# Turning layer-norm rows by VectorE blocks and SBUF copies instead of TensorE transposes, and two heads' probabilities by one VectorE instruction, in a cross-attention block

## The chip, the cores and the metric

One core of one Trainium2 chip runs the whole kernel. The metric is the device time of one execution in microseconds (us). TensorE multiplies, VectorE and ScalarE work on tiles in SBUF and PSUM, GpSimd does a few additions, and SyncE issues nearly all DMA transfers. In the profile these are PE (PEld for its weight loads), DVE, ACT, POOL and SP (SPq for what SP's own queue does).

## The reference

Four sequences, each with 512 query rows x and 512 context rows, width 512, 16 heads of 32, all in fp32. The mask is all true in these inputs, but it is applied.

```python
x = layer_norm(hidden_states, ln1_w, ln1_b)
q = (x @ q_w + q_b)...; k = (enc @ k_w + k_b)...; v = (enc @ v_w + v_b)...
scores = where(mask, q @ k.T * scale, mask_value)
out = softmax(scores) @ v
hidden = out @ cproj_w + cproj_b + hidden_states
y = layer_norm(hidden, ln2_w, ln2_b)
y = gelu(y @ fc_w + fc_b) @ proj_w + proj_b          # inner width 2048
return hidden + y
```

layer_norm is the usual one: mean and variance over the 512 columns, then a weight and a bias per column.

## The kernel before

**Units.** The attention part has 16 groups w = 4b + g: sequence b, four heads g. Each group has four query tiles qt of 128 rows; unit u = 4w + qt. For each unit, TensorE computes the scores of four heads into one PSUM tile (`scores`, line 279); VectorE adds the mask and takes the minimum of the negated scores by row (284); ScalarE takes the exponential and the row sum (288); and VectorE turns the probabilities in 32x32 blocks into a tile tb (`turn`, lines 302 and 310). Two units make a pair, p = 2w + half. After a pair's second unit, 16 copies, 32 partitions each, carry its blocks from tb to the transposed tile pT (`copies`, line 345); `attend` (362) multiplies pT by v, and VectorE scales the result (367).

**One pT.** Pairs 1, 3, 5, 7 and 25 to 31 have buffers of their own (in gt and xe). All others share one tile pT: the copies of the next such pair are emitted just after the attend that frees it. Pairs 8 to 23 attend at the start of unit 2p + 4, so pair 9 at unit 22, pair 16 at 36, pair 23 at 50.

**Other work in between.** After scores and turn, each unit runs some chains of about 3.4 us of TensorE: projections of k, q and v for later groups (kN, qN, vN for group N; lines 235, 245, 257), the output projection cproj of the previous sequence (403), and parts of its MLP (fc at 469, proj at 479). What runs where is written out by hand in the lists `first` and `later`: a tuple gives each unit its own list, while a plain list is spread over the four units by cost in the loop at the end (`run` takes work while what is spent plus half the next cost fits the budget). Transposes are counted at 0.5 each.

**Order.** The schedule is manual: each engine executes what the program emits, in order, and waits in order. SyncE's queue too: a DMA that waits for a tile holds all DMAs emitted after it, weights, rows of x and the copies of pairs among them.

**Layer norms.** There are eight: the first norm of each sequence (giving xT, the input of q), and the second (giving yT, the input of fc). For each: statistics and normalisation by rows in four tiles (`ln_stat`, `ln_rs`, `ln_norm`; lines 145 to 167), then `ln_turn`: 16 TensorE transposes (176) into four PSUM tiles, and weight and bias on the way out, by VectorE (179) or ScalarE (181). The normalised tiles come from a pool of four, which also holds the loaded rows of x (`load_x`, line 194), of h for the next residual (`load_h`, 391) and of the second norm's input (`load_xn`, 412). In the attention part the norms are turned in unit 20 (first norm of sequence 2), 21 to 23 (second norm of 0), 32 to 34 (first of 3) and 46, 47 (second of 1); the second norms of 2 and 3 are turned in the last part (`last_mlps`), each between the second and the third product of a projection, after which the sums over yT (line 501, ys) follow.

Of the kernel before, what the change touches and what calls it, by code (L numbers as in the profile page):

```python
# [1 line left out]

# [9 lines left out]
F32 = mybir.dt.float32  # L38
U8 = mybir.dt.uint8
AF = mybir.ActivationFunctionType  # L40
# [5 lines left out]
P = 128  # L46
B, L, D, H = 4, 512, 512, 16
HD = D // H
INNER = 4 * D
NT = L // P  # L50
ND = D // P
NG = ND
HG = H // NG
# [3 lines left out]
NI = P // HD  # L57
# [15 lines left out]
LN1W, LN1B, QB, KB, LN2W, LN2B, FCB = 0, 4, 8, 12, 16, 20, 24  # L73
# [4 lines left out]
def xattn_block(ctx: ExitStack, tc: tile.TileContext, x, encT, mask, q_w, k_w, v_w, c_w, fc_w, p_w, vecs, rows, out):  # L78
    nc = tc.nc
    scale = float(np.float32(1.0) / np.sqrt(HD).astype(np.float32))  # L80

    def pools(stack, **bufs):
        return [stack.enter_context(tc.tile_pool(name=n, bufs=k)) for n, k in bufs.items()]

    const, keep, hids, tiles, small = pools(ctx, const=1, keep=1, hids=6, tiles=4, small=4)
    dram = ctx.enter_context(tc.tile_pool(name="dram", bufs=1, space=bass.MemoryType.DRAM))
    ps_acc = ctx.enter_context(tc.tile_pool(name="ps_acc", bufs=4, space=PSUM))

# [34 lines left out]
    def score_tile():  # L123
# [2 lines left out]
        n = n // 2 * 4 + n % 2  # L126
        return ptt[:, n * D : (n + 1) * D]

    def kqv_w(w, i):
        n = 4 * i + 2 + w % 2  # L130
        return ptt[:, n * D : (n + 1) * D].rearrange("p (d f) -> p d f", d=ND)

    S = {}
    count = [0, 0, 0]
    Q = [nc.sync]

    def acc_tile(name):
# [33 lines left out]
    def ln_turn(key, d, xn, dst):  # L171

        w, bi = (LN1W, LN1B) if key[0] == 1 else (LN2W, LN2B)
        tp = acc_tile(f"tp{key[0]}_{key[1]}_{d}")
        for t in range(NT):
            nc.tensor.transpose(tp[:, ts(t, P)], xn[t][:, ts(d, P)], ident)
        wd, bd = vec[:, w + d : w + d + 1], vec[:, bi + d : bi + d + 1]
        if d in (1, 2) and key not in BY_ACT:
            nc.vector.tensor_scalar(dst[:, d, :], tp, wd, bd, ALU.mult, ALU.add)
        else:  # L180
            nc.scalar.activation(dst[:, d, :], tp, AF.Identity, bias=bd, scale=wd)


    def queue(b):
        return Q[0] if b else nc.sync

    def load_enc(b):
        for d in range(ND):
            queue(b).dma_start(out=eT[:, d, :], in_=encT[b, ts(d, P), :])

    def load_x(b):
        S["xn", b] = [tiles.tile([P, D], F32, tag="xn", name=f"xn1_{b}_{t}") for t in range(NT)]
        for t in range(NT):
            queue(b).dma_start(out=S["xn", b][t], in_=x[b, ts(t, P), :])

# [76 lines left out]
    def scores(w, qt):  # L272
        if qt == 0:
            S["sums", w] = small.tile([P, NT, HG], F32, tag="sums", name=f"sums_{w}")
        qT, kT, sums = S["qT", w], S["kT", w], S["sums", w]
        sc = ps_sc.tile([P, HG, L], F32, tag="sc", name=f"sc_{w}_{qt}")
        for h in range(HG):
            r = slice(h * HD, (h + 1) * HD)
            nc.tensor.matmul(sc[:, h, :], qT[r, ts(qt, P)], kT[r, :], start=True, stop=True)  # L279
        ps = []  # L280
        for h in range(HG):
            s = score_tile()
            mn = small.tile([P, 1], F32, tag="mn", name=f"mn_{w}_{qt}_{h}")
            nc.vector.tensor_tensor_reduce(  # L284
                out=s, in0=sc[:, h, :], in1=S["mb", w // NG], scale=1.0, scalar=FMAX,
                op0=ALU.add, op1=ALU.min, accum_out=mn,
            )
            nc.scalar.activation(s, s, AF.Exp, bias=mn, scale=-1.0, accum_out=sums[:, qt, h : h + 1])  # L288
            ps.append(s)
        S["ps", w, qt] = ps  # L290

    def turn(w, qt):

        half, q = divmod(qt, 2)
        if q == 0:


            S["tb", w, half] = two.tile([P, NI, PW + 2 * HD], F32, tag="tb", name=f"tb_{w}_{half}")
        tb = S["tb", w, half]
        tv = tb[:, :, :PW].rearrange("p j (a t h q) -> p a h t j q", a=2, t=NT, h=HG)  # L300
        for h in range(HG - q):
            nc.vector.transpose(tv[:, q, h], S["ps", w, qt][h])  # L302
        if q == 0:
            return

        rs = small.tile([P, 2, HG], F32, tag="rsum", name=f"rsum_{w}_{half}")
        nc.vector.reciprocal(rs, S["sums", w][:, 2 * half : 2 * half + 2, :])
        rr = one.tile([P, 2, HG, HD], F32, tag="rr", name=f"rr_{w}_{half}")
        nc.scalar.copy(rr, rs[:, :, :, None].broadcast_to([P, 2, HG, HD]))
        nc.vector.transpose(tv[:, q, HG - 1], S["ps", w, qt][HG - 1])  # L310
        nc.vector.transpose(
            tb[:, :, PW:].rearrange("p j (a q) -> p a j q", a=2), rr.rearrange("p a h d -> p (a h d)")
        )
        waiting.append((w, half))
        if w < NW - 1 or half == 0:
            exchange()
# [59 lines left out]
    def stays(b, t):  # L376

        return b == 0 or b == SPLIT and t < 2

    def load_h(b, *ts_):  # L380

        if ("xa", b) not in S:
            S["xa", b] = dram.tile([L, D], F32, tag=f"xa{b}", name=f"xa{b}")
        for t in ts_:
            if b == B - 1:

                S["h", b, t] = k_q(t // 2, t % 2)
            else:
                pool, tag = (hids, "hid") if stays(b, t) else (tiles, "xn")
                S["h", b, t] = pool.tile([P, D], F32, tag=tag, name=f"h_{b}_{t}")  # L390
            Q[0].dma_start(out=S["h", b, t], in_=x[b, ts(t, P), :])
            if stays(b, t):
                S["hid", b, t] = S["h", b, t]
# [14 lines left out]
    def load_xn(b):  # L408

        for t in range(NT):  # L410
            S["h", b, t] = tiles.tile([P, D], F32, tag="xn", name=f"hn_{b}_{t}")
            Q[0].dma_start(out=S["h", b, t], in_=S["xa", b][ts(t, P), :])

    def load_hid(b, ts_):
# [10 lines left out]

    def norm2(b, t):
        h = S["h", b, t]
        y = tiles.tile([P, D], F32, tag="xn", name=f"xn2_{b}_{t}") if stays(b, t) else h
        S.setdefault(("yn", b), {})[t] = y
        ln_norm((2, b), t, y, h)  # L430

# [2 lines left out]
            if stays(b, t):  # L434
                add_row(S["hid", b, t], 1)

    def ln2_turn(b, d):
        if d == 0:
            S["yT", b] = keep.tile([P, ND, L], F32, tag="yT", name=f"yT_{b}")
        ln_turn((2, b), d, S["yn", b], S["yT", b])  # L440


    weights, products = [], []
# [268 lines left out]
    CHAIN, TURN = 3.4, 0.5  # L712

    def do(fn):
        return [(0.0, fn)]

    def A(w):
        if w >= NW:
            return []
        return [  # L720
            (CHAIN, lambda: prep_k(w)),
            (CHAIN, lambda: prep_q(w)),
            (CHAIN, lambda: prep_v(w)),
        ]

    def C(b):
        return [(CHAIN, lambda t=t: cproj(b, t)) for t in range(NT)]

    def turns1(b):
        return [(TURN, lambda d=d: ln1_turn(b, d)) for d in range(ND)]  # L730

    def turns2(b):
        return [(TURN, lambda d=d: ln2_turn(b, d)) for d in range(ND)]

    def FC(b, q):
        return [(CHAIN, lambda f=f: fc(b, f)) for f in range(q * FQ, (q + 1) * FQ)]
# [3 lines left out]

    def inputs(b):
        ln = [(0.0, lambda part=part: ln1(b, part)) for part in range(3)]
        return do(lambda: load_x(b)), ln, turns1(b), do(lambda: load_enc(b))

    def run(work, budget=None):

# [62 lines left out]
    def some(n):  # L809
        taken, mlp[:n] = mlp[:n], []  # L810
        return taken
# [4 lines left out]
    def h_(b, *ts_):  # L816
        return do(lambda: load_h(b, *ts_))
# [4 lines left out]
    def pb_(b):  # L822
        return do(lambda: proj_bias(b))

    def rs(b):
        return do(lambda: ln_rs((2, b)))

    def stat(b, *ts_):
        return do(lambda: [stat2(b, t) for t in ts_])

    def norm(b, *ts_):
        return do(lambda: [norm2(b, t) for t in ts_])


    x1, x2, x3, x4 = inputs(2)
    k, q, v = A(7)
    c, t2 = C(0), turns2(0)
    first[4] = x1 + [k, q, v] + x4
    later[4] = c[:1] + x2[:1] + c[1:2] + x2[1:2] + c[2:3] + x2[2:] + c[3:]
    k, q, v = A(8)  # L840
    first[5] = (
        [k] + stat(0, 0, 1, 2, 3) + rs(0) + x3 + norm(0, 0, 1, 2, 3) + [v], [q] + t2, some(2) + pb_(0), some(2)
    )
    k, q, v = A(9)
    x1, x2, x3, x4 = inputs(3)
    first[6] = [k, q] + some(4) + [v] + x1
    k, q, v = A(10)
    first[7] = [k, q] + x2[:1] + some(2) + x2[1:2] + some(3) + [v]

    k, q, v = A(11)  # L850
    first[8] = h_(1, 0, 1) + x2[2:] + [k, q] + x3[:2] + some(1) + x3[2:3] + [v] + x3[3:] + h_(1, 2, 3) + x4
    later[8] = cb(1) + C(1)
    k, q, v = A(12)
    first[9] = [q] + some(2) + [k] + some(2) + [v]
    k, q, v = A(13)
    first[10] = [k, q] + some(4) + [v]
    k, q, v = A(14)
    t2 = turns2(1)
    first[11] = (
        [k, q] + stat(1, 0, 1, 2, 3) + rs(1), some(2) + norm(1, 0, 1, 2, 3), some(1) + t2[:2] + [v],  # L860
        t2[2:] + pb_(1) + some(1) + h_(2, 2, 3, 0, 1)
    )

# [101 lines left out]
```

## Time and profile before

| | |
|---|---|
| time, three runs | 809.81, 810.5, 810.87 us; median 810.5 |
| the profiled execution | span 810.8 us from its first to its last instruction; the page gives no other time of it |
| TensorE | 794.0 us busy (98%) |
| VectorE, ScalarE, GpSimd | 556.1 (69%), 359.8 (44%), 98.5 us (12%) |
| SyncE's DMA queue (q1) | 132.43 MB, 61.3% of 16 DMA engines' time |
| layer-norm transposes (line 176) | 128 |
| turns of probabilities (lines 302, 310) | 224 of mean 683 ns, 32 of 656 ns, each 128 x 512 |
| pair copies (line 345) | 504 from SyncE, 8 from ScalarE, 136 KB each |

Lines of the timeline read: start, duration, engine, line, operation, out<-in, count, and in brackets the idle time before with what ended it; the chain of waits has start, duration, what. A line of the windows holds a stretch and its length, busy time (and instructions) of PE, PEld, DVE, ACT and POOL, the granted TensorE clock, the DMA engines' busy share and GB/s. A line for one source line has the shortest, median and longest duration in ns, and the first and last start.

### The profile page before, as it was taken

Reading aid. Unit: us, or ns where it says so; the run is one execution under the profiler, and the core shown is the slowest. Engines: PE = TensorE matmul, PEld = TensorE weight load, DVE = VectorE, ACT = ScalarE, POOL = GpSimd, SP = SyncE. Lnnn points to the kernel's source line nnn. Section 1 sums busy time; section 2 is a strip of 40 time slices with the busy share of each in tenths; the row PEclk is TensorE's granted clock in tenths of the full one; section 3 lists DMA queues with packets and bytes.
Section 4 is the critical chain, followed back from the end, with each engine's and each line's share of the span. In section 5 each row is a group of like instructions: output and inputs, shape, how many; then the busy total and the mean of one; then the engine's idle time right before and its main releaser. Section 6 shows DMA issues by size and latency. Waiting matters only on the chain.

```text
span 810.8 us, 11918 instructions
## 1 busy us (share of the span) xinstructions
PE 794.0 (98%) x4082; PEld 482.1 (59%) x4082; DVE 556.1 (69%) x1273; ACT 359.8 (44%) x785; POOL 98.5 (12%) x112
## 2 busy tenths in 40 slices
PE   9999999979999999999999999999999999999998
PEld 6545445444354544535554333445888888888887
DVE  3779998876678765867778998636738993358511
ACT  2557765537673646546644469700312330023200
POOL 1110030030000030001131000120050021200011
PEclk9999999989999999999999999999999999999999
DMA  9899999937797877778668798883335330023001
GB/s 332 277 236 221 236 223 243 243 92 186 186 240 173 229 202 201 168 196 210 165 144 219 192 266 222 214 247 127 97 111 175 111 116 14 27 79 91 1 14 39
DMA packets 60956, 137.14 MB, mean 169 GB/s; under 512 B 12464, under 2 KB 15664, under 8 KB 60768
## 3 DMA queue, kind: packets, MB, share of 16 engines
q1 hardware_dynamic: 59472, 132.43, 61.3%
q0 software_dynamic: 896, 2.82, 1.0%
q10 hardware_dynamic: 528, 1.14, 0.6%
q8 instruction: 32, 0.52, 0.3%
q14 instruction: 28, 0.23, 0.1%
HBM read 58.22 MB, written 6.82 MB: 80 GB/s over the span
## 4 chain that ended last, share of the span: by engine, by line
PE 82%; DVE 7%; SPq 4%; ACT 3%; DMA 3%; issue 1%; POOL 0%; DVEq 0%; POOLq 0%; ACTq 0%
PE q L573 15%; PE accf L469 7%; PE accc L403 7%; PE sc L279 7%; PE acck L235 6%; PE av L362 6%; PE accp L479 6%; PE accv L257 6%; PE accq L245 6%; SPq L345 4%; DVE ptt L284 2%; PE q5p L613 2%; PE q3p L613 2%; PE q7p L613 2%; PE q2p L613 2%; PE q6p L613 2%
## 5 line engine op out<-in xcount | busy, mean ns | idle before, releaser
L288 ACT ACTIVATE ptt<-ptt,mn 128x512 f32<-128x512 f32 x256 | 181.6, 711 | 134.2 <-DVE mn L284 134.1
L284 DVE CUSTOM_DVE_ANT_0 ptt<-sc,mb 128x512 f32<-128x512 f32 x256 | 161.1, 685 | 47.5 <-PE sc L279 47.4
L302 DVE STREAM_TRANSPOSE tb<-ptt 128x512 f32<-128x512 f32 x224 | 142.0, 683 | 5.5 <-ACT ptt L288 5.1
L469 PE MATMUL accf<-yT,pbt 128*128 128x512 f32 x192 | 87.3, 602 | 0.0
L479 PE MATMUL accp<-pbt,gt 128*128 128x512 f32 x192 | 86.7, 600 | 0.3 <-DMA pbt<-p_w_dram 0.3
L279 PE MATMUL sc<-pbt 32*128 32x512 f32 x512 | 73.7, 645 | 5.2 <-ACT pbt L248 2.7
L573 PE MATMUL q<-ys,gt 128*128 128x256 f32 x320 | 75.1, 379 | 0.0
L573 PEld LDWEIGHTS q<-ys,gt 128*128 128x128 f32 x320 | 60.9, 190 | 8.2
L469 PEld LDWEIGHTS accf<-yT,pbt 128*128 128x128 f32 x192 | 35.0, 190 | 50.2 <-issue 45.4
L479 PEld LDWEIGHTS accp<-pbt,gt 128*128 128x128 f32 x192 | 35.2, 190 | 49.3 <-issue 45.6
L257 PEld LDWEIGHTS accv<-ptt,xe 128*128 128x128 f32 x512 | 58.9, 192 | 8.2 <-issue 6.9
L257 PE MATMUL accv<-ptt,xe 128*128 128x128 f32 x512 | 60.5, 277 | 0.0
L245 PE MATMUL accq<-xe,ptt 128*128 128x512 f32 x128 | 59.3, 607 | 0.0
L235 PE MATMUL acck<-xe,ptt 128*128 128x512 f32 x128 | 59.3, 606 | 0.0
L573 PE MATMUL q<-yT,gt 128*128 128x256 f32 x240 | 58.1, 380 | 0.5 <-DVE gt L501 0.5
L403 PE MATMUL accc<-wc,oT 128*128 128x512 f32 x128 | 56.6, 596 | 0.0
L269 POOL TENSOR_TENSOR v<-v,row 128x512 f32<-128x512 f32 x16 | 20.4, 1272 | 281.4 <-ACT v L262 281.3
L577 ACT ACTIVATE ga<-uc,vec 128x256 f32<-128x256 f32 x40 | 20.3, 508 | 75.5 <-DVE uc L551 75.5
L573 PEld LDWEIGHTS q<-yT,gt 128*128 128x128 f32 x240 | 45.6, 190 | 7.4 <-DVE gt L501 0.9
L362 PE MATMUL av<-pT,v 128*32 128x256 f32 x768 | 48.1, 393 | 1.5 <-DMA pT<-tb 1.5
L584 ACT COPY p<-q 128x256 f32<-128x256 f32 x20 | 7.1, 353 | 92.0 <-PE q L573 92.0
L288 ACT ACTIVATION_READ_ACCUMULATOR ptt<-ptt,mn 128x1 f32 x256 | 47.8, 187 | 0.0
(121 smaller groups left out, 940.4 us busy)
## 6 DMA issues: line engine op xcount, KB each, us to landing
pT<-tb SPq DMA_DIRECT2D x384, 136.0 KB, 2.4
pbt<-p_w_dram SPq DMA_DIRECT2D x40, 256.0 KB, 3.2
gt<-fc_w_dram SPq DMA_DIRECT2D x40, 256.0 KB, 2.7
gt<-tb SPq DMA_DIRECT2D x64, 136.0 KB, 2.8
xe<-tb SPq DMA_DIRECT2D x56, 136.0 KB, 3.1
pbt<-fc_w_dram SPq DMA_DIRECT2D x24, 256.0 KB, 4.7
ptt<-k_w_dram SPq DMA_DIRECT2D x16, 256.0 KB, 3.8
xe<-encT_dram SPq DMA_DIRECT2D x16, 256.0 KB, 4.3
```

The lines of the kernel that those rows point to most:

```text
L235: nc.tensor.matmul(acc, S["wk", w][:, d, :], eT[:, d, :], start=(d == 0), stop=(d == ND - 1))
L245: nc.tensor.matmul(acc, S["wq", w][:, d, :], xT[:, d, :], start=(d == 0), stop=(d == ND - 1))
L257: nc.tensor.matmul(acc[:, ts(t, P)], eT[:, d, ts(t, P)], S["wv", w][:, d, :], start=(d == 0), stop=(d == ND - 1),)
L279: nc.tensor.matmul(sc[:, h, :], qT[r, ts(qt, P)], kT[r, :], start=True, stop=True)
L284: nc.vector.tensor_tensor_reduce(out=s, in0=sc[:, h, :], in1=S["mb", w // NG], scale=1.0, scalar=FMAX, op0=ALU.add, op1=ALU.min, accum_out=mn,
L288: nc.scalar.activation(s, s, AF.Exp, bias=mn, scale=-1.0, accum_out=sums[:, qt, h : h + 1])
L302: nc.vector.transpose(tv[:, q, h], S["ps", w, qt][h])
L362: nc.tensor.matmul(av[ts(h, HD), : 2 * P].rearrange(shape, **kw), v[:, t, ts(h, HD)], p[t][h], start=(t == 0), stop=(t == NT - 1),)
L403: nc.tensor.matmul(acc, S["oT", b][:, g, ts(t, P)], wc[:, g, :], start=(g == 0), stop=(g == NG - 1))
L469: nc.tensor.matmul(acc, S["fcw", b, f][:, d, :], S["yT", b][:, d, :], start=(d == 0), stop=(d == ND - 1))
L479: nc.tensor.matmul(acc, gT[q % 2][:, k, ts(t, P)], S["pw", b, q * FQ + k], start=(k == 0), stop=(k == FQ - 1))
L573: nc.tensor.matmul(o, a[:, k], y[:, k], start=(k == 0), stop=(k == 1))
```

## The change

Six of the eight layer norms (the first norms of sequences 2 and 3, all four second norms) no longer use `ln_turn`. Three steps take its place. `ln_flip`: VectorE turns the four normalised tiles in 32x32 blocks into the destination (xT or yT), used as scratch. `ln_swap`: 16 copies from SyncE carry blocks of 32 partitions x 512 columns (64 KB) from there into the place of the normalised tiles, now one tile xnt. `ln_affine`: ScalarE reads xnt and writes the destination with weight and bias, one instruction per 128 columns of the width. The pool of four tiles becomes slices of xnt, given out in turn by `xn_tile`.

In `turn`, one VectorE instruction turns two heads (128 x 1024) where there were two of 128 x 512; in the second unit of a pair, the reciprocal of the sums stands after the first such instruction.

The lists are written anew: the last cproj of sequence 0 goes from `later[4]` to unit 20, flip, swap and affine stand in units 20, 20 and 21 (first norm of 2), 22, 22 and 23 (second of 0), in group 8's list (first of 3), and in units 46, 46 and 47 (second of 1); v9 moves to unit 22, k9 and q9 to unit 23, and seven MLP chains to group 6. The new steps count as cost 0.

```diff
@@ -82,7 +57,7 @@
     def pools(stack, **bufs):
         return [stack.enter_context(tc.tile_pool(name=n, bufs=k)) for n, k in bufs.items()]
 
-    const, keep, hids, tiles, small = pools(ctx, const=1, keep=1, hids=6, tiles=4, small=4)
+    const, keep, hids, small = pools(ctx, const=1, keep=1, hids=6, small=4)
     dram = ctx.enter_context(tc.tile_pool(name="dram", bufs=1, space=bass.MemoryType.DRAM))
     ps_acc = ctx.enter_context(tc.tile_pool(name="ps_acc", bufs=4, space=PSUM))
 
@@ -126,12 +101,24 @@
         n = n // 2 * 4 + n % 2
         return ptt[:, n * D : (n + 1) * D]
 
+    def score_pair():
+
+        n = (count[2] - 1) % 6 // 2 * 4
+        return ptt[:, n * D : (n + 2) * D]
+
     def kqv_w(w, i):
         n = 4 * i + 2 + w % 2
         return ptt[:, n * D : (n + 1) * D].rearrange("p (d f) -> p d f", d=ND)
 
+    xnt = const.tile([P, NT * D], F32, tag="xnt", name="xnt")
+
+    def xn_tile():
+        n = count[3] % NT
+        count[3] += 1
+        return xnt[:, n * D : (n + 1) * D]
+
     S = {}
-    count = [0, 0, 0]
+    count = [0, 0, 0, 0]
     Q = [nc.sync]
 
     def acc_tile(name):
@@ -181,6 +168,30 @@
             nc.scalar.activation(dst[:, d, :], tp, AF.Identity, bias=bd, scale=wd)
 
 
+    def ln_flip(key, xn, dst):
+
+        tmp = dst.rearrange("p d l -> p (d l)").rearrange("p (j c t q) -> p t c j q", j=NI, c=ND, t=NT)
+        for t in range(NT):
+            nc.vector.transpose(tmp[:, t], xn[t])
+
+    def ln_swap(dst):
+
+        tmp = dst.rearrange("p d l -> p (d l)").rearrange("p (j n) -> p j n", j=NI)
+        for d in range(NI):
+            for i in (0, 2, 1, 3):
+                j = (i + d) % NI
+                nc.sync.dma_start(out=xnt[ts(j, HD), ts(i, D)], in_=tmp[ts(i, HD), j])
+
+    def ln_affine(key, dst):
+
+        w, bi = (LN1W, LN1B) if key[0] == 1 else (LN2W, LN2B)
+        raw = xnt.rearrange("p (i c t q) -> p c t i q", i=NI, c=ND, t=NT)
+        for d in range(ND):
+            nc.scalar.activation(
+                dst[:, d, :].rearrange("p (t i q) -> p t i q", t=NT, i=NI), raw[:, d], AF.Identity,
+                bias=vec[:, bi + d : bi + d + 1], scale=vec[:, w + d : w + d + 1],
+            )
+
     def queue(b):
         return Q[0] if b else nc.sync
 
@@ -189,7 +200,7 @@
             queue(b).dma_start(out=eT[:, d, :], in_=encT[b, ts(d, P), :])
 
     def load_x(b):
-        S["xn", b] = [tiles.tile([P, D], F32, tag="xn", name=f"xn1_{b}_{t}") for t in range(NT)]
+        S["xn", b] = [xn_tile() for t in range(NT)]
         for t in range(NT):
             queue(b).dma_start(out=S["xn", b][t], in_=x[b, ts(t, P), :])
 
@@ -277,7 +288,6 @@
         for h in range(HG):
             r = slice(h * HD, (h + 1) * HD)
             nc.tensor.matmul(sc[:, h, :], qT[r, ts(qt, P)], kT[r, :], start=True, stop=True)
-        ps = []
         for h in range(HG):
             s = score_tile()
             mn = small.tile([P, 1], F32, tag="mn", name=f"mn_{w}_{qt}_{h}")
@@ -286,8 +296,8 @@
                 op0=ALU.add, op1=ALU.min, accum_out=mn,
             )
             nc.scalar.activation(s, s, AF.Exp, bias=mn, scale=-1.0, accum_out=sums[:, qt, h : h + 1])
-            ps.append(s)
-        S["ps", w, qt] = ps
+            if h % 2:
+                S["ps", w, qt, h // 2] = score_pair()
 
     def turn(w, qt):
 
@@ -298,8 +308,9 @@
             S["tb", w, half] = two.tile([P, NI, PW + 2 * HD], F32, tag="tb", name=f"tb_{w}_{half}")
         tb = S["tb", w, half]
         tv = tb[:, :, :PW].rearrange("p j (a t h q) -> p a h t j q", a=2, t=NT, h=HG)
-        for h in range(HG - q):
-            nc.vector.transpose(tv[:, q, h], S["ps", w, qt][h])
+        two_heads = [(tv[:, q, 2 * k : 2 * k + 2], S["ps", w, qt, k]) for k in range(HG // 2)]
+        for k in range(HG // 2 - q):
+            nc.vector.transpose(*two_heads[k])
         if q == 0:
             return
 
@@ -307,7 +318,7 @@
         nc.vector.reciprocal(rs, S["sums", w][:, 2 * half : 2 * half + 2, :])
         rr = one.tile([P, 2, HG, HD], F32, tag="rr", name=f"rr_{w}_{half}")
         nc.scalar.copy(rr, rs[:, :, :, None].broadcast_to([P, 2, HG, HD]))
-        nc.vector.transpose(tv[:, q, HG - 1], S["ps", w, qt][HG - 1])
+        nc.vector.transpose(*two_heads[-1])
         nc.vector.transpose(
             tb[:, :, PW:].rearrange("p j (a q) -> p a j q", a=2), rr.rearrange("p a h d -> p (a h d)")
         )
@@ -386,8 +397,7 @@
 
                 S["h", b, t] = k_q(t // 2, t % 2)
             else:
-                pool, tag = (hids, "hid") if stays(b, t) else (tiles, "xn")
-                S["h", b, t] = pool.tile([P, D], F32, tag=tag, name=f"h_{b}_{t}")
+                S["h", b, t] = hids.tile([P, D], F32, tag="hid", name=f"h_{b}_{t}") if stays(b, t) else xn_tile()
             Q[0].dma_start(out=S["h", b, t], in_=x[b, ts(t, P), :])
             if stays(b, t):
                 S["hid", b, t] = S["h", b, t]
@@ -408,7 +418,7 @@
     def load_xn(b):
 
         for t in range(NT):
-            S["h", b, t] = tiles.tile([P, D], F32, tag="xn", name=f"hn_{b}_{t}")
+            S["h", b, t] = xn_tile()
             Q[0].dma_start(out=S["h", b, t], in_=S["xa", b][ts(t, P), :])
 
     def load_hid(b, ts_):
@@ -425,7 +435,7 @@
 
     def norm2(b, t):
         h = S["h", b, t]
-        y = tiles.tile([P, D], F32, tag="xn", name=f"xn2_{b}_{t}") if stays(b, t) else h
+        y = xn_tile() if stays(b, t) else h
         S.setdefault(("yn", b), {})[t] = y
         ln_norm((2, b), t, y, h)
 
@@ -434,10 +444,14 @@
             if stays(b, t):
                 add_row(S["hid", b, t], 1)
 
-    def ln2_turn(b, d):
-        if d == 0:
+    def ln2_turn(b, step):
+        if step == 0:
             S["yT", b] = keep.tile([P, ND, L], F32, tag="yT", name=f"yT_{b}")
-        ln_turn((2, b), d, S["yn", b], S["yT", b])
+            ln_flip((2, b), S["yn", b], S["yT", b])
+        elif step == 1:
+            ln_swap(S["yT", b])
+        else:
+            ln_affine((2, b), S["yT", b])
 
 
     weights, products = [], []
@@ -729,8 +743,15 @@
     def turns1(b):
         return [(TURN, lambda d=d: ln1_turn(b, d)) for d in range(ND)]
 
+    def flips1(b):
+        return [
+            (0.0, lambda: ln_flip((1, b), S["xn", b], xT)),
+            (0.0, lambda: ln_swap(xT)),
+            (0.0, lambda: ln_affine((1, b), xT)),
+        ]
+
     def turns2(b):
-        return [(TURN, lambda d=d: ln2_turn(b, d)) for d in range(ND)]
+        return [(0.0, lambda n=n: ln2_turn(b, n)) for n in range(3)]
 
     def FC(b, q):
         return [(CHAIN, lambda f=f: fc(b, f)) for f in range(q * FQ, (q + 1) * FQ)]
@@ -740,7 +761,7 @@
 
     def inputs(b):
         ln = [(0.0, lambda part=part: ln1(b, part)) for part in range(3)]
-        return do(lambda: load_x(b)), ln, turns1(b), do(lambda: load_enc(b))
+        return do(lambda: load_x(b)), ln, turns1(b) if b < 2 else flips1(b), do(lambda: load_enc(b))
 
     def run(work, budget=None):
 
@@ -834,30 +855,31 @@
 
     x1, x2, x3, x4 = inputs(2)
     k, q, v = A(7)
+    k8, q8, v8 = A(8)
+    k9, q9, v9 = A(9)
     c, t2 = C(0), turns2(0)
     first[4] = x1 + [k, q, v] + x4
-    later[4] = c[:1] + x2[:1] + c[1:2] + x2[1:2] + c[2:3] + x2[2:] + c[3:]
-    k, q, v = A(8)
+    later[4] = c[:1] + x2[:1] + c[1:2] + x2[1:2] + c[2:3] + x2[2:]
     first[5] = (
-        [k] + stat(0, 0, 1, 2, 3) + rs(0) + x3 + norm(0, 0, 1, 2, 3) + [v], [q] + t2, some(2) + pb_(0), some(2)
+        x3[:1] + c[3:] + stat(0, 0, 1, 2) + [k8] + x3[1:2], stat(0, 3) + rs(0) + x3[2:] + [v8],
+        norm(0, 0, 1, 2, 3) + t2[:1] + [q8, v9] + t2[1:2], t2[2:] + pb_(0) + [k9, q9]
     )
-    k, q, v = A(9)
     x1, x2, x3, x4 = inputs(3)
-    first[6] = [k, q] + some(4) + [v] + x1
+    first[6] = some(7) + x1
     k, q, v = A(10)
     first[7] = [k, q] + x2[:1] + some(2) + x2[1:2] + some(3) + [v]
 
     k, q, v = A(11)
-    first[8] = h_(1, 0, 1) + x2[2:] + [k, q] + x3[:2] + some(1) + x3[2:3] + [v] + x3[3:] + h_(1, 2, 3) + x4
+    first[8] = h_(1, 0, 1) + x2[2:] + [k, q] + x3[:1] + some(1) + x3[1:2] + [v] + x3[2:] + h_(1, 2, 3) + x4
     later[8] = cb(1) + C(1)
     k, q, v = A(12)
-    first[9] = [q] + some(2) + [k] + some(2) + [v]
+    first[9] = [q] + some(3) + [k] + some(2) + [v]
     k, q, v = A(13)
     first[10] = [k, q] + some(4) + [v]
     k, q, v = A(14)
     t2 = turns2(1)
     first[11] = (
-        [k, q] + stat(1, 0, 1, 2, 3) + rs(1), some(2) + norm(1, 0, 1, 2, 3), some(1) + t2[:2] + [v],
+        [k, q] + stat(1, 0, 1, 2, 3) + rs(1), some(2) + norm(1, 0, 1, 2, 3), t2[:1] + some(1) + [v] + t2[1:2],
         t2[2:] + pb_(1) + some(1) + h_(2, 2, 3, 0, 1)
     )
```

## The prediction

> **What bounds the kernel now.** I read, in this order, the page's busy shares, the groups by line, the chain of waits, the timelines of TensorE and of SyncE's DMA queue, and the windows.
>
> ```profile
> PE 794.0 (98%) x4082; PEld 482.1 (59%) x4082; DVE 556.1 (69%) x1273; ACT 359.8 (44%) x785; POOL 98.5 (12%) x112
> ```
>
> TensorE idles 17 us of 810.8, so what leaves TensorE's stream shortens the run, unless a wait takes its place. What the transposes cost there stands in the chain of waits, in the last MLPs:
>
> ```profile
> 592.29 1.96 PE tp L176 x16
> ...
> 674.41 1.96 PE tp L176 x16
> ```
>
> Sixteen transposes of one layer norm hold TensorE 1.96 us, 0.122 us each. At the second norm of sequence 0 a stall lies beside them, seen in TensorE's timeline and in the window around it:
>
> ```profile
> 176.05 1.11 PE L176 MATMUL tp<-ident,xn 128*128 128x128 f32 x4 [4.15 <-ACT pbt L248]
> 177.10 3.64 PE L362 MATMUL av<-pT,v 128*32 128x256 f32 x32
> ...
> 170.00:180.00 10.00, 5.31 (x43) 3.07 (x45) 7.30 (x17) 5.37 (x12) 3.00 (x3) 0.69 0.09 28
> ```
>
> TensorE waits 4.15 us, and then the clock is below full (0.69 on average): the attend takes 3.64 us where others take 1.94, the four transposes 1.11 where others take 0.6. The slow clock costs another 2.3.
>
> Now SyncE's queue, which issues nearly every DMA in program order, waits included: three stretches, then all issues of line 345 and their landing.
>
> ```profile
> 155.62 10.99 SPq L345 DMA_DIRECT2D pT<-tb  x16
> ...
> 268.77 10.03 SPq L345 DMA_DIRECT2D pT<-tb  x16
> 278.84 1.08 SPq L391 DMA_DIRECT2D h<-x_dram  x2
> 281.95 0.33 SPq L461 DMA_DIRECT2D pbt<-fc_w_dram  x1
> 288.31 10.02 SPq L345 DMA_DIRECT2D pT<-tb  x16
> 299.75 1.85 SPq L189 DMA_DIRECT2D xe<-encT_dram  x4
> ...
> 392.15 10.06 SPq L345 DMA_DIRECT2D pT<-tb  x16
> 402.57 1.78 SPq L391 DMA_DIRECT2D h<-x_dram  x4
> ...
> L345 SPq DMA_DIRECT2D pT<-tb x384: 507/589/2129, 33.9 to 520.4; - x192
> DMA to landing us min/median/max: 2.3/2.4/7.1
> ```
>
> A pair's sixteen copies hold the queue 10 us. Two attends that read them:
>
> ```profile
> 304.38 1.94 PE L362 MATMUL av<-pT,v 128*32 128x256 f32 x32
> ...
> 421.47 1.94 PE L362 MATMUL av<-pT,v 128*32 128x256 f32 x32 [0.33 <-DMA pT<-tb]
> ```
>
> The second already waits for its copies: here the queue has no slack left. That decides my forecast.
>
> **What goes.** 96 transposes: 3.9 us in the last MLPs (2 x 1.96); in the attention part 1.75 for the first norm of sequence 2 (TensorE's timeline, 159.65 to 161.39), the same for that of 3, 2.2 and 1.9 for the second norms of 0 and 1: 11.5 in all. With them the stall: 4.15, its slow clock 2.3 and 0.54 for the normalised rows, 7.0 us; and the 0.33 at 421. Together 18.8 us that can be won. The TensorE page of the Trainium skill ("TensorE: Matmul & The Clock Gate", Part 4: PE-mode transpose) has about 275 ns for a transpose among other work; 96 of these would be an estimated 26 us, 15 more than the rows give, and my total 15 lower. This trace has 122 ns. The page "VectorE: DVE Perf Modes" (Rules for kernel authors) speaks against the change: for 128x128 it says TensorE, where PSUM will do.
>
> **What comes, per norm.** VectorE turns four tiles: four turns of this shape in a row take 2.48 us (timeline, line 302). ScalarE applies weight and bias four times: 0.73 apart (line 163, four in 2.93). Between them SyncE issues 16 copies of 64 KB. No row has this copy. The nearest is that of line 345: same memory to same memory, 32 rows, twice the bytes; 0.507 us where issues lie apart, 0.589 back to back, plus 0.045 to the next. Bytes hardly count (a 1024 KB load issues in 0.327, a 20 KB load in 0.412). I take 0.55 a copy, 8.8 a norm, landing 2.3 after the last issue: 10.6 from first issue to last landing. Bounds: 0.375 and landing 1.7 (loads and 128 KB stores), so 7.3; 0.635 and 2.4, so 11.9. "DMA: Bandwidth & Descriptors" (section on why a DMA increments its semaphore by 16) gives 512 sequencer cycles a copy before trn3; at 1.2 GHz an estimated 0.43, and my total some 5 us lower; no run here shows that figure.
>
> Each copy stands in SyncE's queue; what is emitted later stands behind it. ScalarE's affine waits for the last landing, with the next exponentials behind it. And since a norm's raw tile is the tile that later loads write, those loads now wait on the affine, in the queue, ahead of the next pair's copies. GpSimd's queue is passed by nothing; its bias rows for h only start later, with their loads. TensorE follows as below, on the clock of the trace before.
>
> **Place A, sequence 2 norm 1 and sequence 0 norm 2 (unit 20 on).** With only three projections in the run work of units 16 to 19, the attend of pair 8 comes to wait for its copies and runs at 150.5 instead of 153.2. Then copies of pair 9, 152.9 to 163.9; one weight load; the swap from 164.5, landed 175.1; first affine 175.9. TensorE does scores 20, cproj, k8, scores 21, v8, attend 9 (at 165.9, after its copies), scores 22, and at 168.9 needs xT for q8: waits 7.0, and I add 2 for the slow clock, as at 176. q8 ends 181.4; v9, scores 23, k9, q9, attend 10, scores 24 reach 196.2. Meanwhile ScalarE: affine to 178.1, v8, exponentials of unit 22 to 182.3; VectorE: turn to 183.6, four norms of 1.03 to 187.7, flip to 190.2; swap landed 200.8; affine 201.5. fc 0 waits 5.3, plus 2 of clock, and ends at 207.0. Before, the same count of chains was done at 199.94. So 7.1 us later (0.5 earlier at the low price, 11 later at the high).
>
> **Place B, sequence 3 norm 1 (unit 33).** Adding up the budgets of run, swap, affine, two loads of h and four of encT now all fall in unit 33, ahead of the copies of pair 16. Swap from 281.65, landed 292.2; affine to 295.1; loads to 298.0; copies to 308.1, landed 309.9. TensorE, 1.75 earlier, comes to attend 16 at 302.7: waits 7.2, plus 2. Against 304.4 that is 7.5 later (4 to 9).
>
> **Place C, sequence 1 norm 2 (units 46, 47).** Swap from 402.3 behind the copies of pair 22, landed 412.9; affine to 415.8; the four h loads, which write the raw tile, to 417.6; copies of pair 23 landed 429.5. TensorE, without transposes, is there at 419.4: 10.1 of wait plus 2. Against 421.5 that is 10.0 later (7 to 11.5).
>
> **The last MLPs.** Swap of sequence 2 from 592.4, affine done 605.8; the sums over yT, now at 609.5, come no earlier than 607.5. Covered, by 1.7 us; the second project is twice as long. Gain 3.9. Without cover each would cost its excess, at most 2.
>
> **Two heads by one instruction.** 128x512 takes 683 ns, 128x256 takes 415 (line 311): 1.05 ns a column, so 128x1024 about 1.22 us against 1.37, but in a row turns start 0.62 apart and only 0.02 to 0.09 is saved. VectorE saves 0 to 19 us; TensorE waited for line 284 only 2.5. The first pair waits for the second exponential, 0.9 later, but the reciprocal after it waits for the last one anyhow. I take 0, from -2.5 to +2.
>
> **Sum.** +7.1 +7.5 +10.0 -3.9 = +20.7. The profiled execution's span, 810.8, stands 0.3 above the median 810.5, so 831. Low price: -0.5 +4 +6.7 -3.9 = +6.3, 817. High price 11 + 9 + 11.5 - 3.9 = +27.6, and with 3 instead of 2 for each of four slow clocks 842.
>
> **Rivals.** *Faster:* the swaps fit into gaps of the queue (between copies it often idles, as from 170.2 to 181.3 before) and TensorE never waits: 810.5 - 18.8 = 792. It turns on one price, the time from a swap's first issue to the affine's end. The new waits I count, clock included, are 17 at A, 9 at B, 12 at C; below 18.8 in sum the change wins. At 7.3 us from issue to landing I still find some 25, so a swap would have to land in about 5; sixteen issues at the least row, 0.33, take 5.3 before any landing. Chance 0.12, for steps of my walk that may not hold. *Same:* waits and gains cancel, 809 to 812: 0.03. *One place covered,* most likely fc 0 in A, where two norms stand in one chain: 812 to 817, 0.07. *Forecast,* 817 to 842 and a tail above it: 0.78.
>
> A measurement of this kernel tells 0.2% (1.6 us) from no change. Faster 0.12, same 0.03, slower 0.85. The range leaves out the faster and the equal case and about 0.05 above 842: 813 to 842.
>
> **What would show it.** Right: TensorE idle before q8 of the ninth projection, before the first fc, and before attends 16 and 23 with the copies as releaser; window clocks below 1 there; SyncE's swap issues near 0.55 us; no wait of TensorE in the last MLPs except for VectorE's sums. Wrong: swap issues of 0.3 or less; the copies of pair 23 starting before 412; TensorE's idle total staying under 25 us.

## The result, and the profile after

| | before | after |
|---|---|---|
| time, median of four runs | 810.68 us (809.81 to 813.12) | 848.78 us (848.14 to 849.37) |
| ratio | | 1.0467, interval 1.045 to 1.0484 |
| profiled execution, span | 810.8 us | 847.0 us |
| mean granted TensorE clock | 0.994 | 0.972 |

The change makes the kernel 38 us slower; the forecast was 20.7 slower, and 848.78 lies 6.8 above the upper end of its range. The time of a profiled execution is about 1.8 above its span in every kernel below. So the span of 810.8 that the sum started from belongs to an execution some 2 us above the median, and the spans, which differ by 36.2, are what the sum has to be compared with.

The page after, TensorE's busy share and the granted clock by slices:

```profile
PE 790.1 (93%) x3986; PEld 474.6 (56%) x3986; DVE 556.3 (66%) x1159; ACT 365.0 (43%) x793; POOL 97.8 (12%) x112
...
PEclk9999999978999996999996999999999999999999
```

TensorE is busy 3.9 us less, with 96 fewer instructions, and idle 56.9 us instead of 16.8: 40.1 more. 40.1 - 3.9 is the 36.2. The 3.9 is about what is left of the transposes (11.5 us by the prediction's rows) after work at half clock took some 8 back; the digits below 9 are where. The windows around the three places give the granted clock (0.78, 0.83 and 0.80):

```profile
155.00:185.00 30.00, 17.65 (x96) 9.21 (x95) 19.44 (x45) 10.27 (x24) 1.20 (x2) 0.78 0.63 151
300.00:340.00 40.00, 26.55 (x100) 10.57 (x98) 16.04 (x31) 15.93 (x33) 3.60 (x4) 0.83 0.67 173
440.00:475.00 35.00, 22.46 (x114) 10.90 (x113) 15.85 (x32) 14.46 (x35) 7.33 (x7) 0.80 0.66 167
```

The waits of TensorE, grouped (us in total, times, longest):

```profile
PE av L373 <- DMA pT<-tb: 32.7, 4, 13.5
PE accq L256 <- ACT xe L190: 6.3, 1, 6.3
...
PE accf L483 <- ACT yT L190: 4.6, 1, 4.6
```

The two affines (line 190) hold the ninth projection of q and the first fc once each, as the prediction has it, but 32.7 us go to attends whose copies are late. TensorE's timeline shows where:

```profile
150.38 1.93 PE L373 MATMUL av<-pT,v 128*32 128x256 f32 x32 [1.66 <-POOL ve L138]
152.24 1.14 PE L290 MATMUL sc<-pbt 32*128 32x512 f32 x8
153.31 3.70 PE L413 MATMUL accc<-wc,oT 128*128 128x512 f32 x8
...
171.35 3.64 PE L373 MATMUL av<-pT,v 128*32 128x256 f32 x32 [6.06 <-DMA pT<-tb]
...
182.45 5.16 PE L256 MATMUL accq<-xe,ptt 128*128 128x512 f32 x8 [6.29 <-ACT xe L190]
...
206.80 3.78 PE L483 MATMUL accf<-yT,pbt 128*128 128x512 f32 x4 [4.56 <-ACT yT L190]
```

```profile
326.65 3.64 PE L373 MATMUL av<-pT,v 128*32 128x256 f32 x32 [13.45 <-DMA pT<-tb]
...
459.58 3.64 PE L373 MATMUL av<-pT,v 128*32 128x256 f32 x32 [12.54 <-DMA pT<-tb]
```

The attends of pairs 16 and 23, which before waited 0 and 0.33, wait 13.45 and 12.54, and each then runs at half clock (3.64 where 1.94 is usual). The attend of pair 9, at 171.35, waits 6.06, where the prediction's walk leaves about 0.5.

SyncE's queue at places B and C:

```profile
292.38 11.33 SPq L183 DMA_DIRECT2D xnt<-xe  x16
...
308.98 0.81 SPq L401 DMA_DIRECT2D xnt<-x_dram  x2
309.84 1.85 SPq L200 DMA_DIRECT2D xe<-encT_dram  x4
311.80 29.03 SPq L356 DMA_DIRECT2D pT<-tb  x32
...
429.88 10.03 SPq L183 DMA_DIRECT2D xnt<-yT  x16
444.49 1.76 SPq L401 DMA_DIRECT2D xnt<-x_dram  x4
446.30 27.68 SPq L356 DMA_DIRECT2D pT<-tb  x32
```

Swap, then the loads held back until the affine has read xnt (306.02 to 308.97 and 441.52 to 444.46 in ScalarE's timeline), and only then the copies that the next attend needs. And the swap's own issues, all 96 of line 183:

```profile
L183 SPq DMA_DIRECT2D xnt<-yT x64: 512/589/1678, 193.4 to 724.3; - x64
L183 SPq DMA_DIRECT2D xnt<-xe x32: 507/588/596, 170.0 to 303.1; - x32
...
DMA to landing us min/median/max: 2.0/2.0/6.0
```

The chain in the last MLPs shows the one place that won: where sixteen transposes stood between the second and third product, product follows product.

```profile
628.91 3.45 PE q2p L627 x16
632.37 3.45 PE q3p L627 x16
```

### The profile page after: what moved, and what is told of

Its sections match the earlier page's. It is cut to its first block, busy times and chain, and to the rows that moved or that the text cites. A ratio compares the mean times of both kernels' runs of the same rounds, so it can differ in the third digit from the quotient of the medians.

```text
span 847.0 us, 11732 instructions
## 1 busy us (share of the span) xinstructions
PE 790.1 (93%) x3986; PEld 474.6 (56%) x3986; DVE 556.3 (66%) x1159; ACT 365.0 (43%) x793; POOL 97.8 (12%) x112
## 4 chain that ended last, share of the span: by engine, by line
PE 70%; SPq 11%; DVE 9%; DMA 5%; ACT 2%; issue 2%; POOL 0%; DVEq 0%; ACTq 0%; POOLq 0%
PE q L587 14%; PE accf L483 9%; PE accp L493 7%; SPq L356 7%; PE sc L290 5%; PE av L373 5%; PE acck L246 4%; DVE ptt L294 4%; PE accc L413 4%; SPq L183 4%; PE accv L268 3%; PE accq L256 3%; DMA pT<-tb 3%; PE q5p L627 2%; PE q7p L627 2%; PE q2p L627 2%
## 5 line engine op out<-in xcount | busy, mean ns | idle before, releaser
L313 DVE STREAM_TRANSPOSE tb<-ptt 128x1024 f32<-128x1024 f32 x96 | 119.0, 1242 | 45.7 <-ACT ptt L298 42.3
L483 PE MATMUL accf<-yT,pbt 128*128 128x512 f32 x192 | 90.0, 618 | 4.6 <-ACT yT L190 4.6
L373 PE MATMUL av<-pT,v 128*32 128x256 f32 x768 | 51.5, 413 | 35.2 <-DMA pT<-tb 32.7
L483 PEld LDWEIGHTS accf<-yT,pbt 128*128 128x128 f32 x192 | 36.2, 195 | 57.1 <-issue 44.5
L373 PEld LDWEIGHTS av<-pT,v 128*32 128x32 f32 x768 | 25.2, 117 | 63.6 <-issue 46.3
```

The lines of the kernel that those rows point to most:

```text
L313: nc.vector.transpose(*two_heads[k])
L373: nc.tensor.matmul(av[ts(h, HD), : 2 * P].rearrange(shape, **kw), v[:, t, ts(h, HD)], p[t][h], start=(t == 0), stop=(t == NT - 1),)
L483: nc.tensor.matmul(acc, S["fcw", b, f][:, d, :], S["yT", b][:, d, :], start=(d == 0), stop=(d == ND - 1))
```

## The experiments

Medians and ratios to the kernel before, run beside each of them on the same chip (its medians there: 811.67 for the first four, 811.51 for the next four, 811.29 for the last two):

| kernel | median us (range, runs) | ratio, interval | span, clock |
|---|---|---|---|
| pair_only | 809.54 (808.23 to 813.07, 10) | 0.9979, 0.9966 to 0.9993 | 811.3, 0.996 |
| tail_only | 806.41 (805.84 to 809.28, 4) | 0.9943, 0.9921 to 0.9965 | 804.8, 0.996 |
| ot_one | 840.43 (837.16 to 842.65, 4) | 1.0352, 1.0323 to 1.0381 | 838.8, 0.975 |
| loads_late | 829.43 (828.87 to 829.85, 4) | 1.0219, 1.0204 to 1.0235 | 827.1, 0.983 |
| both_fixes | 822.19 (820.23 to 822.76, 4) | 1.0127, 1.0108 to 1.0146 | 820.5, 0.987 |
| both_pool | 811.35 (806.92 to 813.85, 10) | 0.9991, 0.9971 to 1.0011 | 806.7, 0.996 |
| both_split | 805.41 (801.34 to 807.36, 4) | 0.9918, 0.9886 to 0.9951 | 799.6, 1.0 |
| tail_pair | 806.0 (804.95 to 808.76, 5) | 0.9939, 0.9917 to 0.9961 | 805.3, 0.998 |
| split_again | 804.86 (801.51 to 805.31, 6) | 0.9911, 0.9893 to 0.993 | 800.6, 1.0 |
| split_c3 | 804.0 (803.06 to 808.82, 6) | 0.9919, 0.9895 to 0.9943 | 804.1, 0.994 |

The theory that this trace suggests: the loss lies in what stands behind a swap, in SyncE's queue (loads, then copies) and in one buffer, oT. The rivals: the two-head turn makes copies late; or the swap's steps cost by themselves, wherever they stand.

**pair_only**, the kernel before with only the two-head turn:

```diff
-        for h in range(HG - q):
-            nc.vector.transpose(tv[:, q, h], S["ps", w, qt][h])
+        two_heads = [(tv[:, q, 2 * k : 2 * k + 2], S["ps", w, qt, k]) for k in range(HG // 2)]
+        for k in range(HG // 2 - q):
+            nc.vector.transpose(*two_heads[k])
...
-        nc.vector.transpose(tv[:, q, HG - 1], S["ps", w, qt][HG - 1])
+        nc.vector.transpose(*two_heads[-1])
```

> The kernel before, with only the two-head turns. Queue theory (the change loses its time in SyncE's queue, where the norm's 16 copies and the loads that wait for the norm stand ahead of the copies of pairs): the two-head turn is neutral, 809 to 811 us. Rival, turn theory (the turn of two heads, which waits for the second exponential, makes the turned tile late and with it the copies): 815 us or more, and TensorE waits for copies of pairs in several places.

The turn costs nothing and gains at most a little: 0.2%, with an interval that just leaves out 1. Its group in the page:

```profile
L307 DVE STREAM_TRANSPOSE tb<-ptt 128x1024 f32<-128x1024 f32 x96 | 118.8, 1241 | 11.4 <-ACT ptt L292 9.8
```

1241 ns for two heads, where the estimate was 1.22 us and two single turns are 2 x 683. That rival falls for the schedule of before; in the changed schedule the turn was not tried by itself.

**tail_only**, the kernel before with its order and its one-head turns, and flip, swap and affine for the second norms of sequences 2 and 3 alone:

```diff
+FLIP = ((2, 2), (2, 3))
...
     def turns2(b):
-        return [(TURN, lambda d=d: ln2_turn(b, d)) for d in range(ND)]
+        if (2, b) not in FLIP:
+            return [(TURN, lambda d=d: ln2_by_pe(b, d)) for d in range(ND)]
+        return [(0.0, lambda n=n: ln2_turn(b, n)) for n in range(3)]
```

> The kernel before, with flip, swap and affine only for the second norms of sequences 2 and 3, in the last MLPs, where no copies of pairs follow in the queue; one-head turns and the schedule of before. Queue theory: 806 to 807 us, 3.9 less than before, TensorE's idle time as before. Rival, norm theory (the three steps themselves are too long for their cover wherever they stand): 810 us or more, with a wait of TensorE for the sums over yT.

0.57% faster, 4.6 us by the ratio; the transposes there were 3.9. So the three steps are no loss by themselves, which speaks against the second rival: with no copies of pairs and no waiting loads behind them, they are hidden.

**ot_one**, the kernel after with the attention output oT allocated once for all sequences. As a fresh tile of a pool with one buffer it can be written for the next sequence only when every reader of the last one is done; as one tile, each part waits for its own readers.

```diff
-            S["oT", b] = one.tile([P, NG, L], F32, tag="oT", name=f"oT_{b}")
+            if "oT" not in S:
+                S["oT"] = one.tile([P, NG, L], F32, tag="oT", name="oT")
+            S["oT", b] = S["oT"]
```

> The changed kernel with one thing else: the attention output oT is one tile for all sequences, its parts tracked for themselves, where it was allocated anew for each sequence in the same place. cproj 3 of sequence 0, moved behind attend 8, then no longer holds up the product that frees pT. oT theory: the copies of pair 9 start near 153 instead of 157.5 us and TensorE's wait of 6.06 us at attend 9 falls to 1 or 2; total 843 to 845. Rival (those copies are late from the queue and DMA traffic alone): within 1 us of the changed kernel, 848 to 849.5.

What it is about shows in VectorE's timeline, first of the kernel after, then of ot_one. The line is the product that scales the attend of pair 8 and so frees pT for the copies of pair 9:

```profile
149.95 0.67 DVE L414 TENSOR_TENSOR h<-accc,h 128x512 f32<-128x512 f32 x1
157.05 0.42 DVE L378 TENSOR_TENSOR oT<-av,pT 128x256 f32<-128x256 f32 x1 [6.43 <-PE accc L413]
```

```profile
150.51 0.42 DVE L380 TENSOR_TENSOR oT<-av,pT 128x256 f32<-128x256 f32 x1 [1.06 <-PE av L375]
```

In the kernel after, VectorE stands 6.43 us until the last cproj of sequence 0 (153.31 to 157.01 above) has read oT. The change moved that cproj from before the attend of pair 8 to behind it. In ot_one the product comes 6.5 us earlier, and the attend of pair 9 waits 0.82 (TensorE's timeline) instead of 6.06:

```profile
164.25 1.93 PE L375 MATMUL av<-pT,v 128*32 128x256 f32 x32 [0.82 <-DMA pT<-tb]
...
175.28 5.83 PE L256 MATMUL accq<-xe,ptt 128*128 128x512 f32 x8 [8.03 <-ACT xe L190]
```

By the medians 8.4 us less in all (9.3 by the ratios, since the kernel before took 1.0 more on this chip), where 4 to 6 were expected. At the scores of unit 25 TensorE is 8.9 us earlier than in the kernel after; 1.2 of that it had already at unit 19, ahead of anything that oT touches. Of the other 7.7, the waits give 5.4 (6.06 to 0.82 at attend 9, 1.66 to 0.96 at attend 8 and 4.56 to 3.40 at fc, but 6.29 to 8.03 at q), and the clock some 2.5: there is one half-clock stretch less at place A (two, of 10.2 and 3.4 us, for three of 6.8), and 3.9 instead of 6.35 us lost in them.

**loads_late**, the kernel after with the loads of h and of the context rows put behind the next copies in SyncE's queue; no other engine's order changes:

```diff
-    first[8] = ... + [v] + x3[2:] + h_(1, 2, 3) + x4
-    later[8] = cb(1) + C(1)
+    first[8] = ... + [v] + x3[2:]
+    later[8] = h_(1, 2, 3) + x4 + cb(1) + C(1)
...
-        t2[2:] + pb_(1) + some(1) + h_(2, 2, 3, 0, 1)
+        t2[2:] + pb_(1) + some(1)
...
-    first[12] = [k, q], cb(2) + [v], c[:2], c[2:]
+    first[12] = h_(2, 2, 3, 0, 1) + [k, q], cb(2) + [v], c[:2], c[2:]
```

> The changed kernel with only the order of SyncE's queue altered in two places: the loads of h (and encT) that wait for a norm's affine stand behind the copies of pairs 16 and 23 instead of ahead of them. Queue theory: the wait at attend 16 falls from 13.5 to about 5 us and the one at attend 23 from 12.5 to about 6, total 833 to 837. Rival, transport theory (the copies themselves are slowed by other DMA traffic, and order matters little): 846 us or more.

19.4 us less by the medians (20.1 by the ratios), where 12 to 16 were expected. SyncE's timeline at place B, then the two attends in TensorE's:

```profile
288.98 10.99 SPq L183 DMA_DIRECT2D xnt<-xe  x16
300.07 0.53 SPq L239 DMA_DIRECT2D ptt<-v_w_dram  x1
300.69 10.81 SPq L356 DMA_DIRECT2D pT<-tb  x16
311.60 1.01 SPq L401 DMA_DIRECT2D xnt<-x_dram  x2
```

```profile
313.81 2.75 PE L373 MATMUL av<-pT,v 128*32 128x256 f32 x32 [3.70 <-DVE mn L294]
...
438.91 3.64 PE L373 MATMUL av<-pT,v 128*32 128x256 f32 x32 [5.66 <-DMA pT<-tb]
```

The copies follow the swap at once. The waits fall from 13.45 and 12.54 to 3.70 and 5.66, 16.6 us, and with them half-clock time. Not all of the 19.4 is the edit's: of the 19.9 us between the two profiled spans, 3.1 are there already at the scores of unit 28, before anything that it moves, and why is not known. So the order of the queue is worth some 17, about as much as the swap's issues below. (The releaser named for the first, an instruction of VectorE, was long done; the last of the copies landed at 313.35.)

**both_fixes**, both edits together:

> The changed kernel with both edits of the last study, one oT tile and the loads behind the copies. They touch different places, so they should add: 829.4 - 8.3 = 821 us (819 to 823). If it stays at 826 or more, the two were one and the same wait, and the sum of places is wrong.

822.19: the two nearly add up (848.78 - 8.4 - 19.4 is 821.0; by the ratios it is some 2 us short). What is left is 10.7 us above the kernel before, in four waits: q of the ninth projection 7.01, the first fc 4.21, and the attends of pairs 16 and 23 with 3.04 and 6.73. All four stand behind a swap that SyncE issues.

**both_pool** and **both_split**: the swap issued by GpSimd, and by SyncE and GpSimd in turn; both with both edits above.

```diff
-                nc.sync.dma_start(out=xnt[ts(j, HD), ts(i, D)], in_=tmp[ts(i, HD), j])
+                nc.gpsimd.dma_start(out=xnt[ts(j, HD), ts(i, D)], in_=tmp[ts(i, HD), j])      # both_pool
+                (nc.gpsimd if i % 2 else nc.sync).dma_start(out=..., in_=...)                 # both_split
```

> As both_fixes, but the norms' 16 copies are issued by GpSimd instead of SyncE. Queue theory (what is left at attends 16 and 23 is the 10 us that the swap holds SyncE ahead of the copies of pairs): the waits at attends 16 (3.7 us) and 23 (5.7 us) fall below 1.5 each, and with the slow clock after them the total is 806 to 812. Rival, path theory (the norm's own path, flip to affine, holds up ScalarE and with it the turned tiles): both waits stay above 3 and the total is 817 or more. For the waits of q8 and the first fc both give 4 to 9 us and 1 to 5.

> As both_pool, but the 16 copies go in turn to SyncE and GpSimd, eight each. If the issue is what takes the time, the path from flip to affine is some 5 us shorter and the waits of q8 and the first fc fall by 2 to 5 together, while SyncE is held 5 us instead of 10: 806 to 812. If the DMA engines are the limit, the path is as long as before and the total is 814 or more.

both_pool comes out even with the kernel before (the interval holds 1): the pair copies pass the swap, and attend 23 waits 0.73 instead of 6.73; attend 16 still waits 1.99 instead of 3.04, more than the 1.5 expected. But sixteen issues of one engine still take some 8 us (16 x 0.50). Its runs go broadly with the clock, from 0.998 in the one of 806.92 to 0.992 in the one of 813.85. Line 183 in both_split, issues by engine:

```profile
L183 SPq DMA_DIRECT2D xnt<-yT x32: 512/589/939, 182.6 to 671.6; - x32
L183 POOL DMA_DIRECT2D xnt<-yT x32: 496/496/562, 182.8 to 671.3; - x32
...
DMA to landing us min/median/max: 1.8/2.9/7.0
```

Its waits of TensorE, and its clock:

```profile
PE av L375 <- DMA pT<-tb: 2.9, 2, 2.3
PE av L375 <- DMA xnt<-xe: 2.7, 1, 2.7
...
PE accq L256 <- ACT xe L190: 1.1, 1, 1.1
...
core 0: 799.6 us, clock 1.000
```

With half of the swap on each queue the ninth q waits 1.1 us, no wait is over 2.7, and in this execution the clock is never halved (in three others it was 0.994 to 0.996, and the time 804.69 to 807.36). By the medians 16.8 us less than both_fixes, and a little below the 806 to 812 expected. The data and the engines' work are the same in both, so the swap's issues in one queue, with the half clock that the waits bring, were the rest of the loss.

The page "DMA: Bandwidth & Descriptors" of the Trainium skill (Issuing engines are not separate DMA queues) says that DMAs from several engines share the same 16 DMA engines, so that spreading them saves only issue time, usually small beside the DMA itself. Both parts of the first statement show here. A swap takes 5.0 to 9.3 us to issue in both_split instead of 10.0 to 11.3. And in the last swap, where the traces show no other issue among the sixteen, a copy lands 2.0 us after its issue from SyncE alone (the kernel after, 714.84), 1.9 from GpSimd alone (both_pool, 674.91), but 2.6 when both issue in turn (both_split, 667.28; medians). "Usually small" does not hold: beside 10.0 to 11.3 us of issue stand 2.0 from an issue to its landing, and splitting the issues was worth those 16.8 us.

**tail_pair**, tail_only with the two-head turn:

> The two parts that gained, together: flip, swap and affine for the second norms of sequences 2 and 3 alone, and the two-head turns; the schedule and the attention part otherwise as before. Additive: 4.6 + 1.7 less than before, 804 to 806 us, less than both kernels. If the two-head turn's gain was the spread of its runs alone, 806 to 807.

806.0 (ratio 0.9939) beside 806.41 (0.9943) for tail_only: the turn adds nothing that can be told from zero here. As far as the two comparisons show, the turn's gain lies between 0 and 0.3%.

**split_again**, both_split once more with more runs, and **split_c3**, where the last cproj of sequence 0 also goes back to `later[4]`:

```diff
-    later[4] = c[:1] + x2[:1] + c[1:2] + x2[1:2] + c[2:3] + x2[2:]
+    later[4] = c[:1] + x2[:1] + c[1:2] + x2[1:2] + c[2:3] + x2[2:] + c[3:]
...
-        x3[:1] + c[3:] + stat(0, 0, 1, 2) + [k8] + x3[1:2], ...
+        x3[:1] + stat(0, 0, 1, 2) + [k8] + x3[1:2], ...
```

> The same kernel as both_split, for a narrower interval: 805 us (803 to 807), less than the kernel before by 0.5 to 1%. If the first ratio was luck of its rounds, the ratio's interval reaches 1.

> As both_split, with cproj 3 of sequence 0 back in the work of units 16 to 19. It fills the wait before attend 8 (2.3 us in both_split), but takes 3.5 us of TensorE's work from between flip and q8, so the wait of q8 (1.1) grows by about as much: within 2 us of both_split. If TensorE's position at q8 is set by attend 9, that is by the copies of pair 9 and not by the norm, it is 2 us or more below.

split_again stays at 0.9911: this version beats both kernels. split_c3 is the same within the spread. Its wait only moves: q of the ninth projection no longer waits, but the attend of pair 9 does, for 6.98: the copies of pair 9 start at 155.98 instead of 152.40, and the last of them lands at 171.54. So the total does not follow the place of that cproj once oT is one tile.

## Why the prediction was right in direction and short in size

What it read rightly: TensorE bounds, so a wait is what can undo the gain; SyncE's queue has no slack at the copies of pair 23; of the six waits, five are where it put them, four of them with the releaser it named; the last MLPs cover their swaps. By place, in us of TensorE's position (starts of the scores' matmuls, after minus before; within each of A, B and C both kernels run the same number of chains):

| | predicted | measured |
|---|---|---|
| A, scores of unit 19 to 25 | +7.1 | +14.4 |
| B, unit 32 to 37, with the transposes gone | +7.5 | +14.5 |
| C, unit 46 to 51, with the transposes gone | +10.0 | +13.7 |
| last MLPs | -3.9 | -4.7 |
| two-head turn, small shifts in between | 0 | -1.7 |
| sum | +20.7 | +36.2 |

*A: "attend 9 (at 165.9, after its copies)" is the step that failed.* Its walk started the copies of pair 9 at 152.9, right behind the attend of pair 8. They started at 157.50, behind the product that waited 6.43 us for oT. The cproj was followed on TensorE, where its move is free, and not as a reader of a tile with one buffer. The wait came out about 5.6 larger than the 0.5 that the walk implies, and brought a half-clock stretch of its own; ot_one shows it. The waits of q and fc were 6.3 and 4.6 for 7.0 and 5.3. That they came out near is partly luck: the late copies put off both sides, the swap (169.95 instead of 164.5) and TensorE. The attend of pair 8 waited 1.66, as the walk has it.

*B and C: the order was right, the terms too small.* The prediction has the loads wait on the affine ahead of the copies, and loads_late confirms that this is the mechanism. Against its steps, at B: from the swap's first issue to the affine's start 13.6 (292.38 to 306.02) instead of 10.55; the copies' issues 11.3 instead of 10.1; from the last issue's end to the attend 3.6 instead of 1.8, together 6.1 of the 6.25 by which the wait was too small. At C: 11.6 instead of 10.55 and, from the copies' first issue to the attend, 13.3 (446.30 to 459.58) instead of 11.9: all of the 2.4. Two terms, then:

- "I take 0.55 a copy, 8.8 a norm": the median is 0.589, and a swap holds the queue 10.0 to 11.3. The upper bound of 0.635, built from copies of twice the bytes, was the value. The copies stand back to back, so the row for back-to-back copies was the nearest.
- The landing of the copies behind loads. The prediction took the usual 2.3 or less. Behind four context loads issued at once, the first copy of pair 16 landed 6.3 us after its issue and the last 3.9 (the trace's landings): the last of the loads landed at 317.48, only 0.6 before that first copy.

*"I add 2 for the slow clock", four times 8.* Work at half clock cost 1.9, 1.5 and 2.95 at A and 2.8 and 2.85 at B and C: 12.0. (In the kernel before it cost 4.0: the 2.3 at 176, and 1.7 in a stretch of 3.4 us at 51.) The stretches at B and C last 13.7 us each, much of it the wait itself; the work behind it runs slowly to the stretch's end.

"TensorE: Matmul & The Clock Gate" (Part 1) has half clock after an idle window of about 3.4 us. The windows fit: every half-clock stretch in these traces, apart from the one at the end of the run, is 3.4, 6.8, 10.2 or 13.7 us. With every wait of 3.40 (ot_one's fc) or more there comes one, too, within the wait or just after it. But it is no safe limit: waits of 2.67 (both_split) and 3.04 (both_fixes) have none, while stretches of 3.4 come with waits of 2.43 and 1.99 (both_pool), 1.94 (the kernel before, at 51) and 1.63 (loads_late, at 84).

*The transposes.* The prediction sets 122 ns against a page's 275. These are two quantities: in the trace of the kernel before one transpose lasts 273 ns (the median of line 176), close to the 275, but sixteen in a row start 0.11 to 0.12 us apart. The spacing is what leaves TensorE's stream, so the sum was right to use it.

*The rivals.* "Faster" made it turn on one price, the time from a swap's first issue to the affine's end, and asked for a landing in about 5 us. That limit was not the one: in both_split the swaps take 6.7 to 11.5 us from first issue to last landing, and yet the waits of TensorE nearly vanish and the kernel is faster than before. What counted beside the price was what stands behind a swap in SyncE's queue, and it took the two other edits as well. Of the marks named, the swap issues near 0.55, the waits, the low clocks and the clean last MLPs came; those for "wrong" did not. (A slip in the low sum: it takes 6.7 at C, where the walk there gives 7 as the least; the forecast does not rest on it.)

What is left open: why a copy of 32 rows takes 0.589 us to issue whatever its bytes, while loads of 128 rows take 0.33 to 0.46 (medians by line); and why some short waits bring a half-clock stretch and others not. Issuing the swap from ScalarE was not tried.

## What to carry to other kernels

When work is moved from the bounding engine to DMAs, price first the queue that issues them: count the issues back to back, and everything that stands behind them in order, loads that wait on a compute result above all; a load put behind urgent copies was worth some 17 us here, and a second issuing engine 16.8. When an operation is moved past another, ask not only who waits for its output but what it reads, and whether that buffer is about to be written. Start with the places where nothing stands behind the new steps: the two norms at the end gave their 4 to 5 us at once, while the other four lost 43.

## What the hardware showed beyond what was expected

- The issue time of a copy between SBUF tiles does not follow its bytes: 0.507 apart and 0.589 back to back at 64 KB as at 136 KB, both 32 rows. GpSimd issues the same copies in 0.496.
- A copy's landing depends on what is in flight before it: a pair's copy lands 2.4 us after its issue (median before), but 6.3 behind four loads.
- VectorE's 32x32 turn takes 415 ns at 256 columns (float32, 128 rows), 683 at 512 and 1241 at 1024: 1.05 to 1.09 ns a column beside some 0.15 us, an estimate from these three.
